# Two attention layers in fp32: Strassen's seven products for the key and value projections, and the order k, v, q

## The chip, the cores and the metric

The kernel runs on one core of a Trainium2 chip. The metric is the device time of one execution in microseconds (us), with the median over the runs where there are several.

## The reference

The input is one image of 48 x 48 = 2304 tokens with 768 channels. Two layers follow each other, and each adds its result to its input:

```python
x = x + _L0_conv_ref(_gn(x), ...)     # 32 groups of 24 channels, mean and variance over group and image
x = x + _L1_conv_ref(_gn(x), ...)

qkv = x @ qkv_w + qkv_b               # layer 1: qkv_w.T
u = x @ FacTu_w                       # layer 0 only: additions of rank 16 to q and v
new_q = u @ q_facts_w @ FacTv_w * FACT_S
new_v = u @ v_facts_w @ FacTv_w * FACT_S
...                                   # 12 heads of 64 channels
attn = jnp.einsum('bqc,bkc->bqk', q * scale, k)
rel_h = jnp.einsum('bhwc,hkc->bhwk', r_q, Rh)
rel_w = jnp.einsum('bhwc,wkc->bhwk', r_q, Rw)
attn = attn + rel_h[..., :, None] + rel_w[..., None, :]
out = jax.nn.softmax(attn, axis=-1) @ v
return out @ proj_w + proj_b
```

Everything is in float32. Each layer therefore consists of three projections of 2304 x 768 by 768 x 768 (q, k and v), the position terms of q against tables of rows and columns, the attention of 12 heads over 2304 keys, and an output projection of the same size as the other three.

## The kernel before, in words

**Tiles.** Activations are kept with channels on the 128 partitions. `xT` holds a layer's normalised input as 6 blocks (`b`) of 384 tokens by 6 tiles of 128 channels. A matmul takes 128 x 128 weights against 128 x 384 values, and six of them add up in one PSUM tile. In the float32 of this kernel each of them shows in the profile as two records of the MATMUL row. Weights of q, k and v come in halves of 384 output channels (`Weights`, a pool of two buffers, loads issued on SyncE's queue, SP). Where layer 0 adds its low-rank parts, `fold` (L346) multiplies the two factors and adds them onto the weights, six additions on VectorE for each half.

**The projections** (`project`, L365) go half by half, in the order k, q, v. For k and q, `head_rows` (L455) multiplies (L465), adds bias and scale on VectorE (L476), and `store` (L395) splits the result with `in_parts` (L360) into a high part (a cast on ScalarE, L362) and a low part (a subtraction on VectorE, L363), each stored to DRAM through GpSimd's queue (POOL, L402). The first half of k also normalises each block (`normalise`, L235) just ahead of its matmuls. For q it also copies the block in another order of the axes (`columns`, L479 on ScalarE), and the next tile's matmuls are followed by `rel_h` (L416), the position terms by row. The position terms by column (`rel_w`, L437) need the columns of all blocks. They are a Python generator: 16 groups of matmuls into two PSUM buffers, each group copied out by ScalarE or VectorE in turn, and then six pieces that are split and stored. The loop over v's 18 tiles of 128 tokens takes three steps of that generator after each tile:

```python
between = rel_w(half, columns)
for kt in range(NKT):
    ...                                    # six matmuls into ps (L494)
    nc.vector.tensor_add(v, ps, weights.vb[:, ts(half, HP * P)])
    nc.gpsimd.dma_start(vd[half][ts(kt, P), :], v)
    while later:
        later.pop()()
    for _ in range(3):
        next(between, None)
```

The order of the instructions of each engine is the order of the program text. Tiles with the same tag of a pool share its buffers, and a new tile waits until the old one's readers are done.

**The attention** (`attend_plain`, L642) works on 6 pairs of heads and, for each, on blocks of 512 queries (the last has 256), 30 blocks a layer and 60 in all. Keys, queries and position terms are loaded from DRAM on SP's queue (L674, L710, L720, L724), values on POOL's queue (L689). For each of 18 key tiles there are ten matmuls for scores into one of three PSUM buffers, an exponential on ScalarE (L765), a running sum of the exponentials on VectorE (L771), and two matmuls with v, six key tiles behind. At the end of a block the sum is cast into three parts for a matmul that adds it over the keys, `denominators` takes the reciprocal on VectorE (L805), and `finish` (L807) multiplies the result by it and stores it.

**The output projection** (`out_project`, L942) already uses seven products of Strassen's method in Winograd's form: the channels of the weights and the tokens are cut in halves, `sums_of_a` (L898) makes four sums of weight blocks on GpSimd, `sums_of_b` (L905) four sums of blocks of the attention's output on VectorE (L907 to L910). `seven_products` (L913) gives the order of the products and the additions behind them, on ScalarE (copies of two products), VectorE (additions that read PSUM, L921, L924, L1000) and GpSimd (L925, L999). Each product is three matmuls of 128 x 384. The result is added to the residual, and its statistics for the next layer's normalisation are taken (L1004). The projection's weights are loaded on SP's queue into buffers that come free with the projections (L1053).

## Time and profile before

| | us |
| --- | --- |
| median of 3 runs | 3379.43 (3370.71 to 3384.74) |
| the profiled execution | 3374.91 |
| its span (mean granted TensorE clock 0.991) | 3373.1 |
| TensorE busy with matmuls | 3314.2 |
| VectorE busy | 1974.0 |
| ScalarE busy | 1371.2 |
| GpSimd busy | 572.2 |

The profile is of one execution. Its groups of instructions give the line, engine, operation, tiles and number of instructions, then busy time in us and the mean of one in ns, and last the idle time of the engine just before them with what ended most of it. Matmuls are pipelined, so the records of consecutive ones overlap and the mean of one is longer than its share of the time. A timeline shows runs of equal instructions with start, length and, in brackets, the idle time ahead with what released it.

### The profile page before, as it was taken

The page shows a single profiled execution, that of the slowest core. Times are in us where ns is not written, and L with a number is a line of the kernel's source. Part 1 is how long each engine was busy: PE and PEld are TensorE (multiplying, and loading weights), DVE is VectorE, ACT ScalarE, POOL GpSimd, SP SyncE. Part 2 cuts the span into 40 slices and gives each one's busy share as a digit, 9 for nine tenths or more (in the row PEclk, how much of TensorE's full clock was granted, in tenths as well). Part 3 has the DMA queues.
Part 4 walks back from the last instruction along what each step waited for, and adds up shares of the span by engine and source line. Part 5 has one row for each costly group of instructions (what it writes and reads, how often), then busy time and mean ns, then how long its engine had stood idle before and what let it go on. Part 6 is the DMA issues. An engine that isn't in the chain of part 4 may idle for free.

```text
span 3373.1 us, 50177 instructions
## 1 busy us (share of the span) xinstructions
PE 3314.2 (98%) x19924; PEld 2056.4 (61%) x19924; DVE 1974.0 (59%) x1993; ACT 1371.2 (41%) x1501; POOL 572.2 (17%) x905
## 2 busy tenths in 40 slices
PE   8999999999999999999999999999999999999998
PEld 5565665665656666655556656656666666666555
DVE  5332335776777777776543323377777777777742
ACT  2230223555555555553002203245555555555411
POOL 2111124020101010002411212320202010100133
PEclk9999999999999999999999999999999999999999
DMA  6333349262726253534224434764535362625241
GB/s 249 130 130 127 137 149 234 59 154 59 151 62 138 75 125 87 102 80 169 85 90 156 143 117 152 213 144 87 126 81 131 75 134 72 141 62 108 67 162 58
DMA packets 201298, 406.40 MB, mean 120 GB/s; under 512 B 42544, under 2 KB 82768, under 8 KB 197984
## 3 DMA queue, kind: packets, MB, share of 16 engines
q1 hardware_dynamic: 150816, 239.62, 29.7%
q0 software_dynamic: 50240, 163.47, 14.5%
q8 instruction: 161, 2.64, 0.4%
q14 instruction: 81, 0.66, 0.1%
HBM read 254.05 MB, written 148.89 MB: 119 GB/s over the span
## 4 chain that ended last, share of the span: by engine, by line
PE 87%; issue 6%; DVE 2%; DMA 2%; POOL 2%; ACT 1%; SPq 0%; POOLq 0%; DVEq 0%; ACTq 0%
PE ps_sc L739 33%; PE ps_ov L739 25%; PE ps L465 13%; PE psy L989 6%; PE psv L494 6%; DVE sum L771 1%; PE psr L409 1%; PE ps_d L739 1%; PE psc L409 1%; DMA rel<-f_r 1%; DMA xT<-in_x_dram 1%; POOL y L999 0%; DMA q<-f_q 0%; DVE sum L781 0%; POOL f_q L402 0%
## 5 line engine op out<-in xcount | busy, mean ns | idle before, releaser
L765 ACT ACTIVATE pt<-ps_sc 128x1024 f32<-128x1024 f32 (+1 forms) x1080 | 1008.6, 941 | 759.8 <-PE ps_sc L739 685.0
L771 DVE TENSOR_TENSOR sum<-sum,pt 128x1024 f32<-128x1024 f32 (+1 forms) x960 | 1084.0, 1129 | 292.2 <-ACT pt L765 203.5
L739 PE MATMUL ps_sc<-q,k 64*128 64x512 f32 (+1 forms) x8640 | 1094.5, 373 | 12.9 <-ACT pt L765 12.2
L739 PEld LDWEIGHTS ps_sc<-q,k 64*128 64x128 f32 x8640 | 786.0, 186 | 255.5 <-issue 93.1
L739 PE MATMUL ps_ov<-pt,v 128*64 128x512 f32 (+1 forms) x4320 | 885.4, 554 | 1.5 <-DMA v<-f_v 0.9
L739 PEld LDWEIGHTS ps_ov<-pt,v 128*64 128x64 f32 x4320 | 294.2, 137 | 476.8 <-issue 435.7
L465 PE MATMUL ps<-xT,w 128*128 128x384 f32 x1728 | 574.2, 493 | 3.6 <-DVE w L358 1.9
L465 PEld LDWEIGHTS ps<-xT,w 128*128 128x128 f32 x1728 | 330.3, 193 | 226.2 <-issue 6.6
L739 PE MATMUL ps_sc<-rel,places 64*128 64x512 f32 (+1 forms) x2160 | 412.5, 372 | 0.0
L813 POOL DMA_DIRECT2D f_rec<-rec x120 | 59.2, 495 | 1593.3 <-DVE rec L805 1540.8
L494 PE MATMUL psv<-w,xT 128*128 128x384 f32 x864 | 289.2, 491 | 1.9 <-DVE w L358 1.9
L476 DVE TENSOR_SCALAR x<-ps,bt 128x384 f32<-128x384 f32 x144 | 88.9, 618 | 326.3 <-PE ps L465 326.3
L362 ACT CAST xs<-x 128x1152 fp32r<-128x1152 f32 x48 | 55.3, 1151 | 525.9 <-DVE x L476 525.9
L805 DVE RECIPROCAL rec<-ps_d 128x512 f32<-128x512 f32 (+1 forms) x60 | 182.2, 3037 | 105.2 <-PE ps_d L739 105.2
L739 PEld LDWEIGHTS ps_sc<-rel,places 64*128 64x128 f32 x2160 | 212.3, 186 | 27.4
L494 PEld LDWEIGHTS psv<-w,xT 128*128 128x128 f32 x864 | 163.2, 192 | 107.7 <-DVE w L358 3.1
L689 POOL DMA_DIRECT2D v<-f_v x288 | 148.9, 524 | 194.6 <-PE ps_ov L739 152.0
L499 DVE TENSOR_TENSOR v<-psv,vb 128x384 f32<-128x384 f32 x72 | 39.8, 554 | 156.9 <-PE psv L494 141.1
L989 PE MATMUL psy<-oT_t,wproj_s 128*128 128x384 f32 x324 | 113.5, 497 | 5.8 <-DVE oT_t L908 3.6
L780 ACT CAST sum<-sum 128x1024 bf16<-128x1024 f32 (+1 forms) x60 | 57.6, 960 | 143.2 <-DVE sum L771 143.2
L781 DVE TENSOR_TENSOR sum<-sum,sum 128x1024 f32<-128x1024 f32 (+1 forms) x60 | 70.6, 1176 | 61.6 <-ACT sum L780 61.6
L783 DVE TENSOR_TENSOR sum<-sum,sum 128x1024 bf16<-128x1024 f32 (+1 forms) x60 | 68.4, 1140 | 61.6 <-ACT sum L782 61.6
(130 smaller groups left out, 1741.8 us busy)
## 6 DMA issues: line engine op xcount, KB each, us to landing
rel<-f_r SPq DMA_DIRECT2D x1152, 96.0 KB, 4.2
f_k<-xs POOLq DMA_DIRECT2D x48, 576.0 KB, 3.8
f_q<-xs POOLq DMA_DIRECT2D x48, 576.0 KB, 3.7
k<-f_k SPq DMA_DIRECT2D x72, 384.0 KB, 5.7
q<-f_q SPq DMA_DIRECT2D x96, 256.0 KB, 3.2
f_r<-relh POOLq DMA_DIRECT2D x48, 432.0 KB, 5.0
f_r<-relw POOLq DMA_DIRECT2D x48, 432.0 KB, 5.9
w<-in_qkv_w_dram SPq DMA_DIRECT2D x12, 1152.0 KB, 5.8
```

Source lines behind the costliest of these rows:

```text
L409: nc.tensor.matmul(ps[:, i, :, :], lhsT=weights.tables[a][:, 2 * s : 2 * (s + HG)], rhs=lines_of(l0 + i), start=True, stop=True,)
L465: nc.tensor.matmul(ps, lhsT=w[:, t, ts(pr, P)], rhs=xT[:, b, t, :], start=(t == 0), stop=(t == CT - 1),)
L476: nc.vector.tensor_scalar(to, ps, bias, scale, ALU.add, ALU.mult)
L494: nc.tensor.matmul(ps, lhsT=xT[:, kt // TPB, t, ts(kt % TPB, P)], rhs=w_v[:, t, :], start=(t == 0), stop=(t == CT - 1),)
L689: nc.gpsimd.dma_start(v.rearrange("p (b c) d -> p b c d", c=TPB)[ts(i, KG), :, c], found[i, :, :, c],)
L739: in_order(nc.tensor.matmul(*args, **kwargs))
L765: nc.scalar.activation(pt, ps[:, :, 0 : self.n], AF.Exp)
L771: nc.vector.tensor_add(self.sum, self.first if kt == 1 else self.sum, pt)
L781: nc.vector.tensor_sub(self.sum, self.sum, hi)
L783: nc.vector.tensor_sub(lo, self.sum, mid)
L805: nc.vector.reciprocal(self.rec, ps)
L989: nc.tensor.matmul(ps, lhsT=w[left_of][:, t, ts(co, P)], rhs=right[right_of][:, t, :], start=(t == 0), stop=(t == HP - 1),)
```

## The change

The projections are written anew as `project_kv` and `project_q`, in the order k, v, q.

- **k** is made in three thirds of 256 output channels, each in three steps over pairs of token blocks (b and b + 3), with seven products for the four combinations of channel half and block. **v** is made in nine steps (three pairs of blocks by three tiles of 128 tokens), all 768 output channels at once, also by seven products. The four sums of the normalised input (`sums_of_b`) are made once in k's first third, on VectorE, kept in SBUF and used by both.
- The sums of the weights (`sums_of_a`) are a generator of four steps on VectorE, for k's thirds, for v and for the output projection. Those of a third of k are issued at its start (the first at the very start of the layer, beside the last statistics), those of v with its low-rank additions during k's last third, and those of the output projection in the attention, one behind each of four blocks. The output projection's weights are loaded ahead of the attention in the program text.
- k's bias is added in `in_parts`, in an activation on ScalarE and a fused operation on VectorE. Its scale goes to q, in the same manner. Pools of k's split tiles (`part0`, `part1`) hold one buffer each.
- **q** keeps its six-matmul tiles and rel_h. `rel_w` is no generator any more: its 16 groups and six pieces are issued in one go at the end of each half of q, and v's loop no longer stands around it.
- v's bias isn't added to v but to the attention's output, behind the division by the sum of exponentials, as an activation on ScalarE in `finish`. The exponentials' weights sum to one there, so the result is the same.
- `seven_products` takes the products in the order 1, 2, 3, 5, 6, 7, 4, and all its additions, with those of `out_project`, are on VectorE. The output projection of the layer that isn't last has eight PSUM buffers instead of four.

```diff
+    def in_parts(hi, lo, x, scale=None, bias=None):
+
+
+        if bias is not None:
+            nc.scalar.activation(hi, x, AF.Identity, bias=bias)
+            nc.vector.scalar_tensor_tensor(lo, x, bias, hi.bitcast(F32), ALU.add, ALU.subtract)
+        elif scale is not None:
+            nc.scalar.mul(hi, x, scale)
+            nc.vector.scalar_tensor_tensor(lo, x, scale, hi.bitcast(F32), ALU.mult, ALU.subtract)
+        else:
+            nc.scalar.copy(hi, x)
+            nc.vector.tensor_sub(lo, x, hi.bitcast(F32))
...
+    def sums_of_a(a, s1, s2, s4):
+
+        factors = {**a, "s1": s1, "s2": s2, "s3": a["21"], "s4": s4}
+
+        def steps():
+            for op, *args in (
+                (nc.vector.tensor_add, s1, a["21"], a["22"]),
+                (nc.vector.tensor_sub, s2, s1, a["11"]),
+                (nc.vector.tensor_sub, s4, a["12"], s2),
+                (nc.vector.tensor_sub, a["21"], a["11"], a["21"]),
+            ):
+                in_order(op(*args))
+                yield
+
+        return factors, steps()
...
+    def sums_of_b(b, t):
+
+        t1, t2, t3, t4 = (t[:, i] for i in range(4))
+        nc.vector.tensor_sub(t1, b["12"], b["11"])
+        nc.vector.tensor_sub(t2, b["22"], t1)
+        nc.vector.tensor_sub(t3, b["22"], b["12"])
+        nc.vector.tensor_sub(t4, b["21"], t2)
+        return {**b, "t1": t1, "t2": t2, "t3": t3, "t4": t4}
...
+        nc.scalar.copy(p1, product(1))
+        result("11", product(2), p1)
+        p3 = product(3)
+        nc.scalar.copy(p5, product(5))
+        nc.vector.tensor_add(u2, product(6), p1)
+        nc.vector.tensor_add(u4, u2, p5)
+        result("12", p3, u4)
+        nc.vector.tensor_add(u3, product(7), u2)
+        result("22", p5, u3)
+        result("21", product(4), u3)
...
+            def x_factors(b):
+                for i in (b, b + HB):
+                    normalise(i)
+                blocks = {
+                    f"{i + 1}{j + 1}": xT[:, b + j * HB, i * HP : (i + 1) * HP]
+                    for i in range(2) for j in range(2)
+                }
+                t = kv.tile([P, 4, HP, QB], F32, tag=f"t{b}", name=f"xt_{b}")
+                factors.append(sums_of_b(blocks, t))
...
+            def whole():
+                w = kv.tile([P, CT, C], F32, tag="vw", name="w_v")
+                weights.fetch(w, 2 * C)
+                s = kv.tile([P, 3, HP, HP * P], F32, tag="vs", name="w_v_s")
+                sums, steps = sums_of_a(matrix_blocks(w, HP * P), *(s[:, i] for i in range(3)))
+
+                def all_steps():
+                    for half in range(2):
+                        weights.fold(w[:, :, ts(half, HP * P)], 1, half, ps_mm)
+                        yield
+                    yield from steps
+
+                return sums, all_steps()
...
+            everything = slice(None)
+            left, steps = first, ()
+            for g in range(3):
+                for _ in steps:
+                    pass
+                for b in range(HB):
+                    if g == 0:
+                        x_factors(b)
+                    x = kv.tile([P, 2, 2, QB], F32, tag="x", name=f"x_k_{g}_{b}")
+
+                    def result(at, ps, more):
+                        i, j = int(at[0]) - 1, int(at[1]) - 1
+                        to = x[:, i, j]
+                        if not shifted:
+                            to = to.rearrange("p (c i w) -> p i c w", i=8, w=KG)
+                            ps, more = (
+                                y.rearrange("p (i c w) -> p i c w", i=8, w=KG)
+                                for y in (ps, more)
+                            )
+                        nc.vector.tensor_add(to, ps, more)
+
+                    seven_products(kp, QB, multiply(
+                        left, factors[b], everything, everything, False, f"k_{g}_{b}"
+                    ), result)
+                    for i in range(2):
+                        pair = 2 * g + i
+                        half, pr = divmod(pair, HP)
+                        bias = weights.bt[:, CT + pair : CT + pair + 1]
+                        parts = [
+                            kv.tile([P, 2, QB], PART, tag=f"part{n}", name=f"xs_{g}_{b}_{i}_{n}")
+                            for n in PARTS
+                        ]
+                        if shifted:
+                            nc.scalar.activation(parts[0], x[:, i], AF.Identity, bias=bias)
+                        else:
+                            in_parts(*parts, x[:, i], bias=bias)
+                        for to, part in zip(kd[half], parts):
+                            to = to[:, pr, :].rearrange("p (j b q) -> p b j q", j=2, b=HB)
+                            nc.gpsimd.dma_start(to[:, b], part.bitcast(F32))
+
+                    if b == HB - 2 and g < 2:
+                        following = third_of_k(weights, g + 1)
+                    if g == 2:
+                        if b == 0:
+                            following = whole()
+                        for _ in range(3):
+                            next(following[1], None)
+                left, steps = following
+
+            for _ in steps:
+                pass
+            for b in range(HB):
+                for j in range(TPB):
+
+                    place, tag = ((kv, "x"), (vp, "v"))[(b * TPB + j) % 2]
+                    v = place.tile([P, 2, C], F32, tag=tag, name=f"v_{b}_{j}")
+
+                    def result(at, ps, more):
+                        i, k = int(at[0]) - 1, int(at[1]) - 1
+                        nc.vector.tensor_add(v[:, k, ts(i, HP * P)], ps, more)
+
+                    seven_products(kp, QB, multiply(
+                        left, factors[b], everything, ts(j, P), True, f"v_{b}_{j}"
+                    ), result)
+                    for k in range(2):
+                        at = (b + k * HB) * QB + j * P
+                        nc.gpsimd.dma_start(vd[at : at + P, :], v[:, k])
...
+            for half in range(2):
+                w, _ = weights.take("q", half)
+                weights.fold(w, 0, half, ps_mm)
...
+                    store(qd[half], b, x, f"xs_q_{half}_{b}", HD**-0.5)
+                    nc.scalar.copy(
+                        columns[:, :, :, b * lines : (b + 1) * lines],
+                        x.rearrange("p t (h w) -> p t w h", w=HG),
+                    )
+                    later.append(lambda b=b, x=x: rel_h(half, b, x))
+                while later:
+                    later.pop()()
+                rel_w(half, columns)
...
                     nc.vector.tensor_mul(o, self.ps, self.rec)
+                    nc.scalar.activation(
+                        o, o, AF.Identity, bias=v_bias[li][:, self.pair : self.pair + 1]
+                    )
...
+                if i > 1:
+                    next(beside, None)
...
-                        nc.gpsimd.tensor_add(to, to, more)
+                        nc.vector.tensor_add(to, to, more)
...
+        project_q(ly, li, xT, weights, qd, rel_d)
...
-            attend(li, *parts, od)
             w = p3.tile([P, CT, C], F32, tag="w", name="wproj")
             nc.sync.dma_start(w, ly.proj_w.rearrange("(t p) n -> p t n", p=P))
...
+            s = p3.tile([P, 3, HP, HP * P], F32, tag="s", name="wproj_s")
+            w, steps = sums_of_a(matrix_blocks(w, HP * P), *(s[:, i] for i in range(3)))
+            attend(li, qd, kd, vd, rel_d, od, steps)
```

## The prediction, made before the changed kernel had run

> **What bounds the kernel now.** I read the page's list of engines first, then the groups of instructions, the waits of TensorE, and the timelines at the seams between stages.
>
> ```profile
> PE 3314.2 (98%) x19924; PEld 2056.4 (61%) x19924; DVE 1974.0 (59%) x1993; ACT 1371.2 (41%) x1501; POOL 572.2 (17%) x905
> ...
> L465 PE MATMUL ps<-xT,w 128*128 128x384 f32 x1728 | 574.2, 493 | 3.6 <-DVE w L358 1.9
> ...
> L494 PE MATMUL psv<-w,xT 128*128 128x384 f32 x864 | 289.2, 491 | 1.9 <-DVE w L358 1.9
> ```
>
> TensorE is busy 98% of the span and the last column shows almost no idle time ahead of its groups. So fewer matmuls pay in full, if TensorE isn't made to wait elsewhere. The groups' 493 ns are the length of one pipelined record, not its price. The price comes from a stretch of nothing else:
>
> ```profile
> 484.79 0.65 PE L409 MATMUL psc<-columns,tab 128*96 128x144 f32 x4
> 485.28 46.60 PE L494 MATMUL psv<-w,xT 128*128 128x384 f32 x144
> 531.81 1.19 PE L739 MATMUL ps_sc<-q,k 64*128 64x512 f32 x8
> ```
>
> 46.60 / 144 = 0.324 us a record. In this stretch lies what carries my forecast: the last rel_w matmul ends at 485.4 us, the first score starts at 531.8, and v's matmuls fill everything between. What the queue of loads (SP) did meanwhile:
>
> ```profile
> 485.51 0.37 SPq L1053 DMA_DIRECT2D wproj<-in_proj_w_dram  x1
> 507.80 1.75 SPq L674 DMA_DIRECT2D k<-f_k  x2
> 509.84 5.75 SPq L710 DMA_DIRECT2D q<-f_q  x2
> ...
> 524.53 0.30 SPq L724 DMA_DIRECT2D rel<-f_r  x1
> ```
>
> ```profile
> 485.00:532.00 47.00, 47.00 (x150) 27.71 (x150) 14.99 (x20) 6.81 (x6) 20.65 (x36) 1.00 0.94 284
> ```
>
> The first key load goes out only at 507.8, 22.4 us behind the last rel_w matmul: rel_w's six pieces are split into hi and lo and stored, two at a time, because each needs the buffer of the piece two before it. The last bias load of the first group goes out at 524.5 and lands about 4.8 later (529.3). That chain is 44 us long and costs nothing, because v hides it. The last line (time, busy time of PE, PEld, DVE, ACT, POOL, granted clock, DMA share, GB/s) says that the DMA engines are 94% busy in it at 284 GB/s. Layer 1 shows the same: last rel_w matmul 2131.2, key load 2155.1, first score 2178.4.
>
> **What the Trainium skill says.** "TensorE: Matmul & The Clock Gate", section "HAM oscillation — how this bites in real kernels", says that idle gaps of TensorE longer than some 3.4 us drop it to half clock for a while after. The trace agrees:
>
> ```profile
> 1545.48 1.22 PE L739 MATMUL ps_sc<-q,k 64*128 64x256 f32 x8 [4.49 <-ACT pt L765]
> ```
>
> Behind this gap eight records took 1.22 us, 0.64 ahead of it; three such places in the trace lose 1.3 to 3.3 us each on top of the gap. "VectorE: DVE Perf Modes", section "The TRN2 errata — SBUF-src ops pay a fixed extra latency per instruction", gives about (N+151)/0.96 ns for an fp32 addition of two tensors: 557 ns for 384 elements, 1357 for 1152, where the trace has 555 (L921) and 1346 to 1360 (L907 to L910). "ScalarE: Activation LUTs", section "What ACT_TABLE_LOAD costs", prices an activation with a bias at about 280 ns + 0.833 per element, so 0.71 us for 512; the nearest row, the exponential of 1024 elements, takes 1.03. No activation that is added brings a table load into the layers' main path.
>
> **The change, part by part.** All on the profiled run (3374.9 us: span 3373.1 and 1.8 around it), which lies 4.5 us under the median.
>
> (1) *Matmuls removed.* k is half of L465's records, v all of L494's: 1728; seven products for eight leave 7/8: 216 × 0.324 = **−70**. A block of seven products is 42 records, 13.6 us.
>
> (2) *First third of k.* Ahead of and beside each of its three blocks VectorE does 12 normalisations (0.476, L237), 4 sums of 1152 (1.36), 7 additions out of PSUM (0.56 to 0.62) and 2 lo parts of 768 (0.96 by the skill's formula): 5.7 + 5.4 + 4.1 + 1.9 = 17.1 us against 13.6 of TensorE. Six to eight PSUM buffers hide a part: +9 a layer, **+18** (bounds 6 and 30).
>
> (3) *Between k's thirds.* The split parts have one buffer each, so the lo part of a block's second pair stands on VectorE for the store of the first (f_k: 3.8 us to land), and the next third's weight sums stand behind it; product 3 needs the last of these. About 3.5 us, two seams a layer: **+14** (6 to 20).
>
> (4) *Folds.* v's low-rank additions in k's last third, and those of q's second half, which stand on VectorE behind rel_w's splits: **+6** (2 to 12).
>
> (5) *rel_w in a row.* Before, its groups ran between v's tiles. Now q's last x goes through hi (1.15) and columns (2.20) on ScalarE ahead of the first rel_w matmul, covered only by rel_h of the last block: some 4 us of stall. Then 16 groups alternate over two PSUM buffers, 1.87 us for two groups where TensorE needs 1.63: 1.9 more. 6 × 4 halves = **+24** (12 to 30).
>
> (6) *Start of attention, uncovered.* With v ahead of q, rel_w of the second half is TensorE's last work before the scores. The chain that took 44 us now has nothing beside it. v's stores no longer share the DMA engines, so I take 20 for the splits and 18 for the loads, with 1 for the copy: 39 a layer. Floor: wproj 2.36 MB, rel_w 5.3 MB (12 × 442 KB), first keys, queries and biases 2.05 MB, together 9.7 MB / 284 GB/s = 34. The wproj load stays ahead of the keys on SP's queue; v's 24 loads stay on POOL's queue behind the last rel_w store (516.7 before) and are wanted a few us behind the first scores. **+78** (68 to 88). k's and v's own stores go with their blocks to POOL's queue, 36 and 18 a layer with matmuls beside them: nothing, and were POOL late (0.7 us an issue, one block in 13.6), the single part buffers of (3) would show it.
>
> (7) *Bias of v on ScalarE.* 60 activations; each waits for o, which waits for the reciprocal (3.36 us) and stands in ScalarE's queue ahead of exponentials. TensorE has three score buffers, so the next block's scores wait behind those. About half a us where a wide block follows a wide one: **+14** (0: the buffers ride it out; 30: half a us in all 60). The removed bias addition of v (72 × 0.554) was hidden by TensorE and gains nothing.
>
> (8) *Output projection.* Products 1, 2, 3 need no sum or only one of weights; the waits at its starts in both layers (2.2 on POOL and 3.6 on VectorE) go. GpSimd's additions (1.00 to 1.15) become VectorE's (0.56), which has room in that stage (60 of 110 us busy): **−5** (−9 to 0). The weights' sums lie in the attention, four of 1.36 us, hidden.
>
> (9) *First weight sums*, which stand on VectorE ahead of the last statistics until the weights land: **+3** (0 to 6).
>
> (10) *Half clock after the new gaps*: two starts of attention, four rel_w starts and some seams, about eight at 2: **+15** (5 to 28).
>
> Sum: −70 + 18 + 14 + 6 + 24 + 78 + 14 − 5 + 3 + 15 = **+97**. 3374.9 + 97 = 3472; with half of the 4.5 to the median, **3474**.
>
> **Rivals.** *Only the start of attention costs* (no change): the PSUM buffers let TensorE run ahead, so that (2) to (5), (7), (9) and (10) vanish; −70 + 68 − 5 = −7: 3370. For it: TensorE lost only 3.6 us in L465 before, while VectorE normalised there. Against it: stalls in rel_w's chain are in series, no buffer helps.
>
> *The loads run ahead* (faster): the same, and the start of attention takes 15 us a layer, not 39. Splits alone would be 6 × 1.35 on VectorE = 8, and 2.05 MB at 284 GB/s = 7. −70 + 30 − 5 = −45: 3332. It decides once the gap between last rel_w matmul and first score is under some 30 us a layer with nothing else lost. For it: v's stores are out of the way. Against it: the 34 us floor of bytes, unless wproj's 2.36 MB come later.
>
> *VectorE becomes the bound of the projection, and the bias that of attention* (slower still): the upper ends of (2), (3), (5), (7), (10): 3374.9 + 97 + 12 + 6 + 6 + 16 + 13 = 3525.
>
> *The change doesn't do what it says*: if the seven products were not fewer matmuls, the time would be near 3540; the program as built has the smaller count, so this is left out.
>
> **How the numbers follow.** A measurement of this kernel can tell about 0.5%, 17 us. My forecast 0.68, the slower rival 0.15, no change 0.08, faster 0.09. All low ends together give +12 (3387), all high ends +174 (3549). The range that leaves out no more than 2 in 10 is 3370 to 3530: the faster rival (0.09) and the upper half of the slower one (0.07) are outside. Faster 0.09, same 0.08, slower 0.83.
>
> **What would show it.** After: 1512 records of 128x384 for k and v where there were 1728; two gaps on TensorE of 35 to 45 us, one ahead of each layer's first score, ended by the bias loads, with DMA share above 0.9; TensorE's waits for VectorE in k's first third and at its seams of 3 to 4 us; rel_w's matmuls at 1.87 us a pair; exponentials delayed by the activation on o. I am wrong if the gap at the first score is under 25 us, or if waits of the attention grow by more than 30 us.

## The result, and the profile after

The changed kernel takes 3463.44 us (median of 4 runs, 3459.56 to 3470.06), the kernel before 3382.09 beside it: 1.0247 times as long, with a 95% interval of 1.0215 to 1.028. The profiled execution has a span of 3464.9 us, at a mean granted clock of 0.975 where it was 0.991.

The page's list of engines and three of its groups of instructions (busy time and mean, then idle time ahead with what ended most of it):

```profile
PE 3281.5 (95%) x19708; PEld 2011.8 (58%) x19708; DVE 2114.7 (61%) x2267; ACT 1427.5 (41%) x1645; POOL 442.9 (13%) x795
...
L929 PE MATMUL ps_sc<-q,k 64*128 64x512 f32 (+1 forms) x8640 | 1102.4, 374 | 74.4 <-DMA q<-f_q 64.7
...
L510 PE MATMUL ps_k<-xT,w_k 128*128 128x384 f32 x324 | 122.5, 533 | 29.7 <-DVE w_k L404 25.2
```

TensorE has 216 instructions fewer and is less busy, but the idle column is no longer near zero. Two waits stand out at once: the scores wait for the first queries, and k's products for sums of weights. The groups by shape show v's products:

```profile
L510 PE MATMUL ps_v<-w_v,xT 128*128 128x384 f32 x216 | 72.6, 486 | 0.0
L510 PE MATMUL ps_v<-w_v_s,xt 128*128 128x384 f32 x216 | 72.6, 486 | 0.0
L510 PE MATMUL ps_v<-w_v,xt 128*128 128x384 f32 x216 | 72.6, 486 | 0.0
...
L510 PE MATMUL ps_v<-w_v_s,xT 128*128 128x384 f32 x108 | 37.8, 486 | 0.0
```

These are 756 records where v had 864, and no idle time. Layer 0's v takes 122.1 us for its 378 (198.29 to 320.36), 0.323 a record as before. So the matmuls were saved in full. Their place is taken by this, on TensorE's timeline at the start of the first attention:

```profile
522.34 16.26 PE L620 MATMUL psc<-columns,tab 128*96 128x144 f32 x96
571.02 2.58 PE L929 MATMUL ps_sc<-q,k 64*128 64x512 f32 x8 [32.42 <-DMA q<-f_q]
575.17 0.76 PE L929 MATMUL ps_sc<-rel,places 64*128 64x512 f32 x1 [1.58 <-DMA rel<-f_r]
```

The gap of 32.4 us, where v's matmuls had stood, is followed by scores at half clock (the granted clock is 0.50 from 571 to 582 us; eight scores take 2.58 us, 1.19 before) that wait for position terms. In layer 1 the gap is 31.85 us. SP's queue in that time, and the busy times of the gap (PE, PEld, DVE, ACT, POOL, granted clock, DMA share, GB/s):

```profile
538.68 0.37 SPq L1195 DMA_DIRECT2D wproj<-in_proj_w_dram  x1
...
561.46 1.74 SPq L865 DMA_DIRECT2D k<-f_k  x2
566.50 0.80 SPq L900 DMA_DIRECT2D q<-f_q  x2
...
571.92 0.30 SPq L914 DMA_DIRECT2D rel<-f_r  x1
```

```profile
539.00:571.00 32.00, 0.00 (x0) 0.01 (x1) 8.55 (x7) 6.81 (x6) 9.24 (x16) 0.54 0.90 293
```

It is the chain of before, in the same order. No compute engine is busy for even a third of it, and the DMA engines are 90% busy. Where the time went, by stages read from TensorE's timelines of the two profiled executions:

| stage | before, us | after, us | difference |
| --- | --- | --- | --- |
| start to the first projection matmul | 36.7 | 42.4 | +5.7 |
| layer 0: to the first score | 495.1 | 528.6 | +33.5 |
| layer 0: attention, to the last matmul with v | 1040.3 | 1051.6 | +11.3 |
| output projection, to layer 1's first projection matmul | 132.8 | 130.5 | −2.3 |
| layer 1: to the first score | 473.6 | 502.3 | +28.7 |
| layer 1: attention | 1040.0 | 1052.7 | +12.7 |
| output projection, to the last store's issue | 144.5 | 137.3 | −7.2 |
| behind it, to the end of the span | 10.2 | 19.6 | +9.4 |
| sum | 3373.1 | 3464.9 | +91.8 |

### The profile page after: what moved, and what is told of

Same layout as the page of the kernel before. It is cut to its first block, busy times and chain, and to the rows that moved or that the text cites. A ratio compares the mean times of both kernels' runs of the same rounds, so it can differ in the third digit from the quotient of the medians.

```text
span 3464.9 us, 50208 instructions
## 1 busy us (share of the span) xinstructions
PE 3281.5 (95%) x19708; PEld 2011.8 (58%) x19708; DVE 2114.7 (61%) x2267; ACT 1427.5 (41%) x1645; POOL 442.9 (13%) x795
## 5 line engine op out<-in xcount | busy, mean ns | idle before, releaser
L955 ACT ACTIVATE pt<-ps_sc 128x1024 f32<-128x1024 f32 (+1 forms) x1080 | 991.5, 939 | 679.5 <-PE ps_sc L929 618.4
L961 DVE TENSOR_TENSOR sum<-sum,pt 128x1024 f32<-128x1024 f32 (+1 forms) x960 | 1072.7, 1117 | 319.7 <-ACT pt L955 236.2
L674 PE MATMUL ps_q<-xT,w_q 128*128 128x384 f32 x864 | 292.0, 492 | 3.1 <-DVE w_q L371 2.5
L674 PEld LDWEIGHTS ps_q<-xT,w_q 128*128 128x128 f32 x864 | 162.6, 193 | 107.8 <-DVE w_q L371 3.9
L510 PE MATMUL ps_k<-xT,w_k 128*128 128x384 f32 x324 | 122.5, 533 | 29.7 <-DVE w_k L404 25.2
L510 PE MATMUL ps_k<-xt,w_k 128*128 128x384 f32 x432 | 145.9, 494 | 2.2 <-DVE xt L419 1.2
L680 DVE TENSOR_SCALAR x_q<-ps_q,bt 128x384 f32<-128x384 f32 x72 | 44.4, 617 | 142.0 <-PE ps_q L674 141.6
L510 PEld LDWEIGHTS ps_k<-xt,w_k 128*128 128x128 f32 x432 | 83.0, 194 | 64.2 <-issue 4.1
L961 DVE TENSOR_TENSOR sum<-pt 128x1024 f32<-128x1024 f32 (+1 forms) x60 | 67.1, 1118 | 82.1 <-ACT pt L955 81.1
L510 PEld LDWEIGHTS ps_k<-xT,w_k 128*128 128x128 f32 x324 | 66.0, 208 | 81.5 <-issue 22.4
```

What stands on the lines that cost most here:

```text
L510: nc.tensor.matmul(ps, lhsT=y if transposed else x, rhs=x if transposed else y, start=(t == 0), stop=(t == HP - 1),)
L674: nc.tensor.matmul(ps, lhsT=w[:, t, ts(pr, P)], rhs=xT[:, b, t, :], start=(t == 0), stop=(t == CT - 1),)
L680: nc.vector.tensor_scalar(x[:, pr], ps, weights.bt[:, pair : pair + 1], ly.q_scale, ALU.add, ALU.mult,)
L955: nc.scalar.activation(pt, ps[:, :, 0 : self.n], AF.Exp)
L961: nc.vector.tensor_add(self.sum, self.first if kt == 1 else self.sum, pt)
```

## The experiments

All were timed in rounds, each beside the kernel before. Medians are compared with the changed kernel's 3463.4 unless the text says otherwise. That kernel was timed in the first round alone, and the median of the kernel before moved between 3376 and 3382 us from round to round, so a difference of 5 us between two runs says little.

**The order alone (e_before_kvq).** The kernel before with its three projections in the order k, v, q in each half and rel_w in one go behind q, as the change has it, and nothing else:

```diff
-        ORDER = [(mat, half) for half in range(2) for mat in (1, 0, 2)]
+        ORDER = [(mat, half) for half in range(2) for mat in (1, 2, 0)]
...
-                    for _ in range(3):
-                        next(between, None)
+                columns = one.tile([P, HP, HG, HG], F32, tag="columns", name=f"columns_{half}")
+                head_rows(weights.take(0, half, ps_mm), half, 0, ly.q_scale, columns)
+                while later:
+                    later.pop()()
+                for _ in rel_w(half, columns):
+                    pass
```

> The kernel before with only the order changed: in each half k, v, q, and rel_w in one go behind q; matmuls, bias and output projection as before. Theory (the order alone costs what the changed kernel lost at the start of the attention and in rel_w): 32 us of gap and about 9 of slow and waiting matmuls ahead of the first values in each layer, and some 5 us at rel_w: 3376 + 2 x (32 + 9 + 5) = about 3468. Rival (the gap is there only because of other parts, v's new tiles and stores or the pools of the new projections): less than 40 us more than before.

Measured: 3462.71 us, 1.0247 times the kernel before (1.023 to 1.0264). TensorE's waits:

```profile
PE ps_sc L738 <- DMA q<-f_q: 67.6, 4, 33.5
...
PE psr L409 <- DVE relh L363: 7.3, 4, 2.6
PE ps_sc L738 <- DMA k<-f_k: 6.4, 2, 4.1
```

The order alone costs 83 us, as much as the whole change, with the same gap (33.1 and 33.5 us) ahead of the first scores. The rival of under 40 is out. The gap needs neither v's new tiles nor the new pools: it comes with what lies behind rel_w. It also follows that all the other parts of the change together, the 70 us of matmuls among them, came to about nothing on top of it.

**Another order (e_qkv).** The changed kernel with q ahead of k and v; tiles laid out so that the first loads' buffers come free early. With it, k's first weight sums stand in q's second half, v's blocks take the order 2, 0, 1, and the load of the output projection's weights comes later.

```diff
-        ORDER = [("k", 0), ("k", 1), ("k", 2), ("q", 0), ("q", 1)]
+        ORDER = [("q", 0), ("q", 1), ("k", 0), ("k", 1), ("k", 2)]
...
+            first = project_q(ly, li, xT, one, weights, qd, rel_d, normalise)
         with tc.tile_pool(name="p1_kv", bufs=1, **REUSE) as kv:
...
+            project_kv(ly, li, xT, kv, weights, first, kd, vd)
```

> The changed kernel in the order q, k, v: the queries, rel_h and rel_w come first (normalised there), then k by thirds, then v with its token blocks in the order 2, 0, 1; the tiles in SBUF are laid out so that the first keys and queries can be loaded before v is done, and the output projection's weights are loaded behind the second block of the attention. Theory (the start of the attention is what the change lost): k's and v's matmuls now lie between rel_w and the first score, so TensorE's gap of 32 us there in each layer and the 8 to 11 us of slow and waiting matmuls behind it go. 3463 - 2 x (32 + 9) = about 3380, give or take 15, with a gap under 8 us (v's own loads) ahead of or soon behind the first score. Rival (the loss sits in k's weight sums, in the sums of the input on VectorE and in rel_w itself, and the start of the attention only shows it): the order moves the waits into k's first third, where rel_w's split pieces stand on VectorE and ScalarE, and the time stays above 3430.

Measured: 3422.66, so 41 us less, half of what the first theory gave, and between the ranges of the two. TensorE's timeline:

```profile
279.94 10.80 PE L512 MATMUL ps_k<-xt,w_k 128*128 128x384 f32 x24 [15.27 <-DVE xt L415]
...
548.28 1.19 PE L939 MATMUL ps_sc<-q,k 64*128 64x512 f32 x8 [0.17 <-ACT pt L965]
569.78 8.31 PE L939 MATMUL ps_ov<-pt,v 128*64 128x512 f32 x24 [10.90 <-DMA v<-f_v]
```

The gap ahead of the scores is gone (0.17 us). Two new waits stand in its place: k's sums of the input behind rel_w's low parts on VectorE (31.3 us in both layers together), and the first values, whose loads go out only behind v's last store (22.7). Both theories had a part of it: the gap could be removed, and half of it moved.

**Weight sums first (e_sums_first).** One edit in the changed kernel:

```diff
                     ), result)
+                    if b == HB - 1 and g < 2:
+                        for _ in following[1]:
+                            pass
                     for i in range(2):
                         pair = 2 * g + i
```

> The changed kernel, with the weight sums of k's next third issued ahead of the splits of the last block of a third instead of behind them. Theory (the sums are late because VectorE stands at the low part, which waits for a store to free its one buffer): the four waits of TensorE for w_k (25 us) go, and the half clock behind them (some 3 us each): 3463 - 25 - 10 = about 3428. Rival (the low part's wait for the store holds the results of the next products on VectorE as well, so TensorE runs out of PSUM buffers instead): less than 10 us are gained, and TensorE waits for x_k or kept tiles at the same places.

Measured: 3430.44, 33 us less, near the theory's 35. All waits for w_k are gone, and no wait for x_k or kept tiles has come at these places. What they had been is seen on VectorE's timeline of the changed kernel, at the first seam:

```profile
89.08 1.01 DVE L378 SCALAR_TENSOR_TENSOR xs<-x_k,bt,xs 128x768 fp32r<-128x768 f32 x1
90.01 0.55 DVE L537 TENSOR_TENSOR x_k<-ps_k,kept_u 128x384 f32<-128x384 f32 x1
96.31 1.02 DVE L378 SCALAR_TENSOR_TENSOR xs<-x_k,bt,xs 128x768 fp32r<-128x768 f32 x1 [5.76 <-DMA f_k<-xs]
97.25 0.55 DVE L404 TENSOR_TENSOR w_k<-w_k 128x384 f32<-128x384 f32 x1
```

The second low part waits 5.76 us for the store of the first, and the weight sums stand behind it. TensorE resumes 2 us later, at 99.38, and at half clock (0.50 granted up to 103 us).

**v's bias (e_no_vbias).** The activation in `finish` is taken out, so this kernel leaves v's bias out of its result.

```diff
                     nc.vector.tensor_mul(o, self.ps, self.rec)
-                    nc.scalar.activation(
-                        o, o, AF.Identity, bias=v_bias[li][:, self.pair : self.pair + 1]
-                    )
```

> The changed kernel without the activation that adds v's bias to the attention's output; the bias of v is left out of the result. Theory (the activation waits for o in ScalarE's queue, exponentials stand behind it, and TensorE's scores wait for their buffers): the 38 short waits of the scores for the exponential (9.0 us in all) go, and the time falls by 9. Rival (three score buffers ride it out, the waits come from the reciprocal's neighbourhood and remain): within 3 us of the changed kernel. The prediction's 14 would need 0.4 us in each of 36 blocks.

Measured: 3444.32, so 19 us less, more than either expected. The 38 short waits of the scores for exponentials are gone from its trace. A block of the changed kernel shows why, first on ScalarE and then on TensorE:

```profile
1014.89 0.72 ACT L1000 ACTIVATE o<-o,v_bias 128x512 f32<-128x512 f32 x1 [0.85 <-DVE o L999]
1015.52 4.77 ACT L955 ACTIVATE pt<-ps_sc 128x1024 f32<-128x1024 f32 x5
```

```profile
1013.88 1.09 PE L929 MATMUL ps_sc<-q,k 64*128 64x512 f32 x8
...
1015.02 1.09 PE L929 MATMUL ps_sc<-q,k 64*128 64x512 f32 x8
...
1016.58 1.20 PE L929 MATMUL ps_sc<-q,k 64*128 64x512 f32 x8 [0.22 <-ACT pt L955]
```

One key tile's scores follow the last after 1.14 us, the late one after 1.56. The idle column says 0.22, but the pitch has lost 0.42: consecutive records overlap, and a gap also takes the overlap away. The other places are like it, and all 38 are 16 us by their pitch, not the 9.0 that the list of waits adds up.

**The 2.36 MB of the output projection's weights (e_wproj_late, e_wproj_held).** In the first run the load was only moved in the program text:

```diff
-            nc.sync.dma_start(w, ly.proj_w.rearrange("(t p) n -> p t n", p=P))
...
+            def late():
+                nc.sync.dma_start(bt, ly.proj_bt)
+                in_order(nc.sync.dma_start(
+                    whole_w, ly.proj_w.rearrange("(t p) n -> p t n", p=P)
+                ))
+                yield
+                yield
+                yield from sums
```

> The changed kernel, with the load of the output projection's weights (2.36 MB) moved from ahead of the attention to behind its second block. Theory of bytes (the start of the attention is bound by what the DMA engines can move, about 284 GB/s): 2.36 MB less is 8 us less a layer; the gap ahead of the first score falls from 32 to about 24 us, the time by 16. Theory of latency (each split piece waits for the store of the piece two before it, whatever else is on the DMA engines): the gap stays within 2 us of 32, and the time within 5.

Measured: 3463.18. SP's timeline shows that nothing had been tested, since the load still goes out ahead of the keys:

```profile
536.60 0.37 SPq L1202 DMA_DIRECT2D wproj<-in_proj_w_dram  x1
...
558.39 2.10 SPq L865 DMA_DIRECT2D k<-f_k  x2
```

In the second run a copy behind the attention's second block writes a column of the tile first:

```diff
+                if i == 1:
+                    nc.vector.tensor_copy(mark.pop(), block.sum[:, 0, 0:1])
...
+            mark.append(whole_w[:, 0, 0:1])
```

> The changed kernel with the load of the output projection's weights held back by data: a copy behind the attention's second block writes one column of their tile first. (In the run e_wproj_late the load still went out ahead of the keys, so that run tested nothing.) Theory of bytes (DMA engines at 0.85 to 1.0 of their time in the gap): 2.36 MB less is 8 us less ahead of the first score in each layer, 24 for 32, and 16 in the time. Theory of latency (two buffers for the split pieces, each waiting for the store of the piece two before): within 2 us of 32.

Measured: 3458.13; the load goes out at 653.7 us, and the gaps are 29.2 and 30.5 us, 3.2 and 1.3 shorter. Neither theory: bytes would have given 8, latency nothing.

**Three buffers for rel_w's pieces (e_relw3).**

```diff
+            wide = es.enter_context(tc.tile_pool(name="p1_w", bufs=3, **REUSE))
...
-                    bp.tile([P, HP, QB], PART, tag=f"part{i}", name=f"{name}_{i}")[0:rows]
+                    (wide if name.startswith("relw") else bp).tile(
+                        [P, HP, QB], PART, tag=f"part{i}", name=f"{name}_{i}"
+                    )[0:rows]
```

> The changed kernel with three buffers instead of two for rel_w's split pieces. Theory of latency (a piece waits for the store of the piece that had its buffer): the first wait of 7 us on ScalarE and the later ones of 1 to 3 us shrink, the gap ahead of the first score falls from 32 to about 27 us, the time by 10. Theory of bytes (six pieces of 0.88 MB at 284 GB/s are 18.7 us however many buffers there are; with wproj held back the gap was 29 and 30): the gap stays within 2 us of 32.

Measured: 3467.38, with gaps of 34.8 and 33.9 us. The gap's windows in e_wproj_held and e_relw3, columns as above:

```profile
538.40:567.50 29.10, 0.00 (x0) 0.00 (x0) 8.91 (x7) 6.81 (x6) 9.47 (x16) 0.55 0.79 241
```

```profile
537.80:572.50 34.70, 0.00 (x0) 0.00 (x0) 8.82 (x7) 6.83 (x7) 14.11 (x25) 0.56 0.93 287
```

With a third buffer the pieces are split sooner (the key load goes out at 557.1 us, 19 behind the last rel_w matmul, where it was 23), but the loads behind them land no sooner. With fewer bytes the engines are less busy (0.79) and the gap still lasts 29. So neither bytes nor the wait for a buffer sets it alone. That both hold it is likely but not shown: no run changed both at once, and none changed the queue that issues the stores. How the 32 us divide stays open.

**The output projection alone (e_before_out).** The kernel before with products in the order 1, 2, 3, 5, 6, 7, 4 and

```diff
+        nc.vector.tensor_add(u4, u2, p5)
...
-        nc.gpsimd.tensor_add(u4, u2, p5)
...
-                        nc.gpsimd.tensor_add(to, to, more)
+                        nc.vector.tensor_add(to, to, more)
```

> The kernel before with only the output projection's part of the change: products in the order 1, 2, 3, 5, 6, 7, 4 and all their additions on VectorE (sums of the weights still on GpSimd at the start of the stage). The traces have 132.8 and 144.5 us from the attention's last matmul to the next layer's first and to the last store in the kernel before, 130.5 and 137.3 in the changed one: 9 us less together. If order and engine alone make it, 9 us less than before; if the weights' sums being ready at the start make half of it, 4 to 5; rival (VectorE's additions lengthen the tail behind the last product): within 2.

Measured: 0.9973 times the kernel before (0.9964 to 0.9983), 9 us less (6 to 12). So order and engine make most of the gain and perhaps all: by the stages of its profile it is 7.4 us, where the changed kernel has 9.5, and the two were not told apart. (The weights' sums turned out to run inside the attention in the kernel before, too: its trace has them on GpSimd from 564.6 us on.)

**The end of the program (e_vb_read).**

```diff
-            nc.sync.dma_start(v_bias[self.li], ly.qkv_bt[:, 2 * CT :])
+            nc.sync.dma_start(v_bias[self.li], ly.v_b.rearrange("o (t p) -> p (o t)", p=P))
```

> The changed kernel, with v's bias loaded from the input of its own that the kernel before used and the changed one leaves unread; same values, same place. In the profiles 19.6 us lie between the last store's issue and the end of the span where that input is unread (four kernels), 10.2 where it is read (four kernels). Theory (the unread input is what lengthens the end): 9 us less, 3454. Rival (it is only a coincidence with something else of the program's end): within 3 us of 3463.

Measured: 3464.38, and 19.5 us behind the last store's issue. The unread input is not the reason. The 9 us stay unexplained.

**Putting it together (e_best, e_best2, e_best3).** The main edits on top of e_qkv; the activation in `finish` goes too, and the blocks of k and v change their order:

```diff
+            (on or nc.vector).tensor_sub(lo, x, hi.bitcast(F32))
...
+                    if at_b == HB - 1 and g < 2:
+                        for _ in following[1]:
+                            pass
...
+                        nc.vector.tensor_add(to, to, vb[:, ts(i, HP * P)])
...
+                    for b in range(NQB):
+                        for i in range(8):
+                            nc.gpsimd.dma_start(into[ts(i, KG), b], found[i, :, b])
```

> Order q, k, v as in the run e_qkv (3423), with its new waits removed one by one: rel_w's low parts of the second half on GpSimd, so that the sums of the input for k don't stand behind them on VectorE (15.3 and 16.1 us there, and about 3 of half clock each); the weight sums of k's next third ahead of the splits (33 us in its own run); v's bias added to v by VectorE, not to o by ScalarE (19 us in its own run); the first pair's values loaded token block by token block in 48 smaller loads, with v's last blocks chosen so that the values wanted first are stored first (10.9 and 11.8 us). If the costs add up and lie where the traces put them: 3423 - 37 - 33 - 19 - 23 = 3311; I expect 3310 to 3335. Rival (the waits only change places, each uncovering the next): above 3360.

Measured: 3335.74, 0.9871 times the kernel before (0.9855 to 0.9888): 1.3% faster than before and 3.7% faster than the change. The first score follows v's last matmul, and values no longer wait. It is 25 us over the sum of the parts. TensorE's waits say where, in the first and third of these lines (the second, 13.0, was there in the changed kernel too, with 13.5):

```profile
PE ps_k L512 <- ACT kept_p L431: 18.9, 4, 10.0
PE psr L632 <- DVE relh L380: 13.0, 8, 2.6
...
PE ps_k L512 <- DVE w_k L400: 6.9, 2, 6.5
```

The copies of k's first products stand on ScalarE behind rel_w's casts, which wait for stores. The wait has changed engines.

Where e_best gains on the kernel before shows by the stages of the two profiles (3333.8 and 3373.1 us, 39.3 less). Up to the first scores it is 15.8 us shorter in both layers together, and 5.7 longer at the start; the output projections and the end give some 9.5, and the two attentions 19.7. So of the 70 us of matmuls some 16 are left, net of what still waits, in the stages that saved them. Half of the gain lies in the attention; the last section says what the traces show of that.

> The same, with the low parts of rel_w's first half on GpSimd too. Theory (in layer 0 the low-rank additions to q's second half stand behind those on VectorE): 3 us of waits and 3 of half clock go in layer 0, 6 us less than the run e_best. Rival (GpSimd's queue also issues the stores of q and rel_h, which now stand behind 3.5 us operations that wait for stores themselves): the same or up to 10 us more.

```diff
-                    store(rel_d[1][half], b, rel[:, :, ts(b, QB)], f"relw_{half}_{b}", on=nc.gpsimd if half else None)
+                    store(rel_d[1][half], b, rel[:, :, ts(b, QB)], f"relw_{half}_{b}", on=nc.gpsimd)
```

e_best2 takes 3335.75: no difference, as its rival had it. In e_best3 the copies of k's first third change engine:

```diff
-                    ), result)
+                    ), result, nc.vector.tensor_copy if g == 0 else None)
```

> As the run e_best (3336), with the copies of products 1 and 5 in k's first third on VectorE instead of ScalarE. In e_best TensorE waited 18.9 us, at four places, for those copies, which stood on ScalarE behind rel_w's casts that wait for stores. Theory: these waits and the half clock behind the long ones (2 to 3 us in each layer) go, 15 to 25 us: 3311 to 3321. Rival: the split of k's first block still stands behind rel_w's casts on ScalarE, VectorE's low part waits for it, and the results behind that hold TensorE all the same: under 6 us gained.

e_best3 takes 3338.26: no gain either. TensorE's waits for kept copies fell only from 18.9 to 12.4 us, now on VectorE, waits for xt (6.0) came beside them, and that for w_k stayed (5.6, 6.9 in e_best).

## Why the prediction was right, step by step

The change was forecast slower, 3474 in a range of 3370 to 3530; it took 3463. Of the rivals, the one with only the start of attention costing is refuted by the waits for w_k, and the one with loads running ahead by these and by the gaps (32 us, only just above its 30). VectorE is not the bound of the projection either, since moving the sums ahead of a wait removed the loss without less work.

Of the signs that it named, the 1512 records, the two gaps and the exponentials behind the activation on o were seen. The gaps were 32 us and not 35 to 45, their DMA share was 0.90 and 0.92, and what ended them were the first queries; the position terms cost a few short waits more. A pair of rel_w's groups took 2.0 us and not 1.87. Two of its figures are off: its low ends add up to +20 (3395), not +12; and of the sums of L907 to L910, whose means it gives as 1346 to 1360 ns, L908 has 1806, because four of its six took 2.03 us.

1. *Matmuls*, −70: right. v has 108 records fewer (54 a layer), k likewise, and 216 at 0.323 us give −70.
2. *First third of k*, +18: too large. The first 138 records of k take 51.4 us in layer 0 and 50.0 in layer 1, where 138 × 0.324 is 44.7. Half clock at the start, which the kernel before had too, is 2 to 3 of that, so +7 in both layers together. TensorE's waits for VectorE in them are only 3.2 and 2.0 us, so more was hidden than I allowed, by the PSUM buffers as I take it.
3. *Between thirds*, +14: the right mechanism, mis-sized, and past my bound of 20. The seams wait 5.6 to 7.05 us instead of 3.5, and with half clock e_sums_first gave back 33. I took the landing time of one store from the page (3.8). The second pair's high and low part wait for two stores that go out one after the other (at 89.2 and 90.4 us; the low part starts at 96.3), and the sums stand behind both.
4. *Folds*, +6: about right; 3.9 us of waits and 3 of half clock ahead of q's second half in layer 0.
5. *rel_w in a row*, +24: the sum is right, a premise is not. Three halves stall 3.4 us each and take 16.3 to 16.7 us for 96 records that took 13.0 between v's (six in 0.81). In layer 1's first half the order of the text wasn't kept: q's next matmuls stand between the groups, on TensorE's timeline:

```profile
2109.01 0.98 PE L620 MATMUL psc<-columns,tab 128*96 128x144 f32 x6 [0.24 <-ACT relw L660]
2109.82 0.81 PE L674 MATMUL ps_q<-xT,w_q 128*128 128x384 f32 x2
2110.46 1.63 PE L620 MATMUL psc<-columns,tab 128*96 128x144 f32 x12
```

   That half paid 5.5 us in other waits instead. About +26 in all. The description of the kernel above, that each engine follows the program text, is too strict: a later instruction was moved ahead where there was room. The run e_wproj_late fell to the same error; its load was even marked `in_order` and still went out ahead of the keys' loads, which are not marked. What held in e_wproj_held was a dependence.
6. *Start of attention*, +78: right as a sum (64.3 us of gaps, and 7.8 and 11.1 more until the second batch of values, so +83), and e_before_kvq shows it without the rest of the change. The floor of 34 us was no floor: 32.4 and 31.85 were measured, and 2.36 MB less took only 1 to 3 us off.
7. *v's bias*, +14: right in kind, 19 measured. The price of half a us was right; it is paid in 38 places, where 14 allows for 28.
8. *Output projection*, −5: right in kind, −9 measured in e_before_out, my bound. That the weights' sums are hidden in the attention is right for the changed kernel; that they cost the kernel before something there is what I missed (below).
9. *First weight sums*, +3: +5.7 at the start, within the bound; 3.8 of it is the longer wait for the last statistics (4.7 us, 0.9 before).
10. *Half clock*, +15: it is inside (3), (4) and (6) as measured. "TensorE: Matmul & The Clock Gate" in the Trainium skill, section "HAM oscillation — how this bites in real kernels", says that an idle window puts TensorE to half clock; the first scores' 2.58 us for 1.19, with 0.50 granted, agree.

Two things of the size of a term were not in the sum. The end of the program is 9.4 us longer; why is open. And the attention of the kernel before has five waits for exponentials, 12.2 us, that the changed kernel doesn't have (about −13 with what follows them); the traces give a reason, told in the last section. Together: −70 + 7 + 33 + 7 + 26 + 83 + 19 − 9 + 6 + 9 − 13 = +98, where the profiles differ by 91.8; the terms overlap by that much. That the prediction's 97 came so near is partly luck, because the terms missed on both sides: (2) was 11 too large, (3) some 19 too small with its clock, and the two that weren't in it, +9 and −13, nearly cancel.

## What to carry to other kernels

Before a stage is moved, ask what it hides: v's matmuls were not only work but the cover of a 44 us chain of splits, stores and loads, and moving them cost as much in a kernel with no other change. Where an instruction waits for a store, look at what stands behind it on its engine; giving the same sums a place ahead of the two splits was worth 33 us. Seven products for eight did pay once the order put them between rel_w and the first score, but by some 16 us of 70; the rest of e_best's 1.3% comes from the attention and the output projection. And ask what work on one engine does to its neighbours: by the traces, the weights' sums that left GpSimd took 12 us of TensorE's waits with them, for which I had no term.

## What the runs showed of the hardware that I had not expected

A gap on TensorE costs more than its idle time: 0.22 us idle took 0.42 from the pitch of the scores. And VectorE's sums of two tensors take much longer while GpSimd subtracts. VectorE's timeline of e_best:

```profile
261.83 1.35 DVE L416 TENSOR_TENSOR xt<-xT,xt 128x1152 f32<-128x1152 f32 x1
263.10 0.55 DVE L539 TENSOR_TENSOR x_k<-ps_k,kept_p 128x384 f32<-128x384 f32 x1
263.57 3.31 DVE L418 TENSOR_TENSOR xt<-xT,xt 128x1152 f32<-128x1152 f32 x1
266.81 3.99 DVE L415 TENSOR_TENSOR xt<-xT 128x1152 f32<-128x1152 f32 x1
```

GpSimd's subtractions stand at 260.84 to 265.67 and 266.75 to 269.57 there. The sums of the third and fourth line end 1.2 us behind the end of one, which is nearly the 1.3 that they take alone. "SBUF — State Buffer" in the Trainium skill, section "SBUF: two separate sides", says that the two engines share a pair of ports as an exclusive lock, for which an operation with two SBUF inputs on VectorE contends with one on GpSimd that reads SBUF; the first has it for its whole length. The trace agrees from both sides: the first line keeps its 1.35 us, and the subtraction that begins ahead of it, inside another such sum (260.58 to 261.92), took 4.83 us where the five others took 2.6 to 3.2. Work taken off VectorE in e_best thus came back in part as waiting on it.

The attention of the kernel before has the same pattern. Its eight sums of the output projection's weights run on GpSimd there, and the eight sums of exponentials beside them on VectorE take 2.5 to 3.5 us, where one takes 1.23. Ahead of the first of TensorE's two waits of 4.5 us:

```profile
1531.79 9.72 DVE L771 TENSOR_TENSOR sum<-sum,pt 128x1024 f32<-128x1024 f32 x4
1536.81 3.62 POOL L902 TENSOR_TENSOR wproj_s<-wproj,wproj_s 128x1152 f32<-128x1152 f32 x1
1541.55 1.04 ACT L780 CAST sum<-sum 128x1024 bf16<-128x1024 f32 x1 [6.77 <-DVE sum L771]
```

Two of the four sums take 3.48 us. ScalarE's cast waits 6.77 us for them, the exponentials stand behind the cast, and TensorE waits 4.49 us for these (the line at 1545.48 us in the prediction). Four of the five waits, 12.0 us, follow such sums. The change put the weights' sums on VectorE, and no sum of exponentials is longer than 1.4 us any more; e_before_kvq and e_before_out, which keep them on GpSimd, keep the two waits of 4.5 us. No run moved them alone, so this is read from the traces and not shown by an experiment.

Last, 19.6 us lie between the last store's issue and the end of the span in the changed kernel, 10.2 before. It is 10.0 to 11.6 in the six profiles of this study in which GpSimd executes additions or subtractions of tensors, and 19.5 to 19.8 in the eight in which it doesn't. No run changed this alone, so it is a coincidence seen, not a cause shown.
